# Attention layer: the products with the outputs' weights for two heads of both chunks at a time, in 64 columns

## The chip, the cores and the metric

The kernel runs on one core of one Trainium2 chip. Its time is the device time of one launch in microseconds (us), as the median of several runs. The engines of a core are TensorE (PE, with its weight loads shown apart as PEld), VectorE (DVE), ScalarE (ACT), GpSimd (POOL) and SyncE (SP, which here only issues DMA transfers). Each runs its own instructions in order; semaphores join them.

## The reference

Four graph layers follow one another on 6250 nodes of 160 features (64 scalars and 32 vectors of three components) and 100000 edges that are sorted by their destination. The change lies in the first, an attention layer. Cut to what matters:

```python
msg_s = (s_n @ Ws_src)[src] + (s_n @ Ws_dst)[dst]            # msg_v likewise
w1 = rbf @ W_rbf
m1_s, m1_v = _cg_tp(msg_s, msg_v, y0, y1, w1[...])            # products with the edge's y
a = (m1_s @ W_alpha).reshape(e, H, AS_)                       # H = 4 heads
a = jnp.sum(jnp.where(a > 0, a, 0.2 * a) * alpha_dot, axis=-1, keepdims=True)
amax = jax.ops.segment_max(a, dst, num_segments=n)
ex = jnp.exp(a - amax[dst])
den = jax.ops.segment_sum(ex, dst, num_segments=n)
alpha = ex / (den[dst] + 1e-16)
val_s = m1_s @ Ws_val                                         # val_v likewise; both gated by a sigmoid
m2_s, m2_v = _cg_tp(val_s, val_v, y0, y1, w2_...)
h = concat([m2_s @ Ws_vlin, m2_v @ Wv_vlin])                  # per head: 16 scalars, 8 vectors
agg = jax.ops.segment_sum(alpha * h, dst, num_segments=n)     # then a linear map, and a residual
```

## The kernel before, in words

The edges are padded to 784 chunks of 128. A chunk's edges reach few destination nodes: it has a window of 16 nodes (`WM0`). The edge loop of the attention layer, `edge_loop0`, takes four chunks (`WC0`) in each of its 196 steps. For every step there is an object of the class `Window0`, whose methods are the stages of the work; the list `STEP0` gives, for one step, pairs of a lag and a stage. In step s the stage with lag k is done for the chunks of step s - k. The list is written out in the code, and each engine gets its instructions in the list's order; so it is a pipeline of eight steps (lags 0 to 7). PSUM is shared out by `bank`: four banks in turn, 15 times a step, and a bank is given out again when the last reader of its tile is done.

The stages, in the order of the data:
- `edges` and `nodes` gather rows of features by edge and by window (POOL); `ends_load` and `radial_load` bring the destinations of the edges (tile `dn`), and their 16 radial features (`yr`) and factors (`yb`), for four steps at a time, as DMA transfers of SP. `radial_turn` multiplies the latter two (POOL), `masks` compares `dn` with the nodes of the windows (DVE), and `others` turns that into large negative numbers (ACT).
- `ends` and `weights` are products into the tile `wf`; `features`, `dots`, `dot` and `product1` form the message `tp` (DVE and POOL).
- `turn` and `turned` transpose it (PE, then a copy by ACT to `xt`); `linear` multiplies it with `w_m`; `tanh`, `directed`, `crossed`, `joined`, `gates`, `values` and `gated` form the values `val`.
- `channels`, `leak`, `leaky`, `scores` give the scores: a row of `s` for each head and node of a window, a column for each edge. Two chunks share 128 rows, ordered chunk, head, node (2 x 4 x 16). `largest`, `negated`, `exps` and `denominators` are the softmax.
- `by_edge` transposes the exponentials, `weighted` (L1473) multiplies them with the four factors of the edge. `sums` (L1481) and `sums_z` (L1493) sum the values over the edges, for each chunk, head, node and factor; ACT copies them out of PSUM as `a` (`summed`) and `az` (`summed_z`).
- `outputs` (L1512) multiplies `a` and `az` with the weights `w_o`. A product takes 32 columns of `a`, which are two heads of one chunk, as its stationary operand and 80 columns of weights (two heads side by side) as its moving one; five of them are summed into 32 rows of the tile `po`. There are 2 pairs of chunks x 5 x 2 chunks x 2 halves of the heads = 40 of them a step. `even` and `odd` pick the right head's 40 columns of the 80 into `row`.
- `write` (L1536) stores a chunk's rows of `row` to a table in DRAM, at its window's place, which `bases` (L1529) reads into registers of SP: one DMA for each chunk. After each step a part of the later layers' tables is filled with zeros (L1636, SP), as long as there are any left.

A product of 32-bit numbers is two instructions on PE with a weight load each, so a step's 40 products with `w_o` show as 80; transposes are one.

Of the kernel before, what the change touches and what calls it, by code (L numbers as in the profile page):

```python
# [10 lines left out]
F32 = mybir.dt.float32  # L11
I32 = mybir.dt.int32
# [21 lines left out]
ORDER0 = (0, 2, 1, 3)  # L34
# [13 lines left out]
def kernel(ctx: ExitStack, tc: tile.TileContext, t: dict, out: bass.AP):  # L48
# [146 lines left out]

    win0A = const.tile([1, NCH], I32, name="win0A")
# [5 lines left out]
    with tc.tile_pool(name="win", bufs=1) as sb, tc.tile_pool(name="winp", bufs=1, space=PSUM) as ps:  # L202
# [131 lines left out]
        bits = sb.tile([P, 3], I32, name="bits")  # L334
        vec.tensor_scalar(bits[:, 0:1], pi, 15, None, ALU.bitwise_and)
        vec.tensor_scalar(bits[:, 1:2], pi, 6, None, ALU.logical_shift_right)
        vec.tensor_scalar(bits[:, 2:3], pi, 4, 3, ALU.logical_shift_right, ALU.bitwise_and)
        bf = sb.tile([P, 3], F32, name="bf")
        vec.tensor_copy(bf, bits)
        vec.tensor_scalar(slot0[:, 0:1], bf[:, 1:2], float(WM0), bf[:, 0:1], ALU.mult, ALU.add)  # L340
# [11 lines left out]
        for h in range(2):  # L352
            q = slice(S * h, S * h + S)
            vec.tensor_copy(win0F[q, :], nb[q, h:NCH:2])
# [892 lines left out]
    class Window0:  # L1247
# [12 lines left out]
        def __init__(self, w, sb, ps, n, k, radial, dst, gi, y, yc, ids, node_idx, rows, tps):  # L1260
            self.w, self.sb, self.ps, self.n, self.np = w, sb, ps, n, n // 2
            self.k, self.radial, self.dst = k, radial, dst
            self.gi, self.y, self.yc, self.ids, self.node_idx = gi, y, yc, ids, node_idx
            self.rows, self.tps = rows, tps
            self.t, self.z, self.pa = {}, {}, {}
            self.f = self.xt = self.th = self.q = self.val = self.a = None

            self.groups = [(g, c) for g, c in enumerate(ORDER0) if c < n]

# [192 lines left out]
        def by_edge(self):  # L1462

            self.pe = self.bank()
            for p in range(self.np):
                pe.transpose(self.pe[:, p * P : (p + 1) * P], self.pT[:, p, :], ident)
# [16 lines left out]
        def summed(self, p):  # L1483
            if self.a is None:
                self.a = self.sb.tile([P, WC0, 4, S], F32, name="a", bufs=2)
            act.copy(self.a[:, 2 * p : 2 * p + 2].rearrange("p c i m -> p (c i m)"), self.pa[p])

        def sums_z(self):

            self.pz = pa = self.bank()  # L1490
            for c in range(self.n):
                for i in range(4):
                    pe.matmul(  # L1493
                        pa[i * V : (i + 1) * V, c * S : (c + 1) * S], self.val[:, c, P:F], self.py[:, c, i, :], start=True, stop=True
                    )

        def summed_z(self):
            n = self.n
            self.az = self.sb.tile([P, WC0, S], F32, name="az", bufs=2)
            act.copy(self.az[:, 0:n].rearrange("p c m -> p (c m)"), self.pz[:, 0 : n * S])  # L1500

        def outputs(self):

            w = self.w["o"]
            self.po = po = self.bank()[:, 0:160].rearrange("p (a k) -> p a k", a=2)
            for p in range(self.np):
                for i in range(5):
                    for h in range(2):
                        for g in range(2):
                            q = slice(h * S + g * 32, h * S + g * 32 + 32)  # L1510
                            x = (self.a[:, 2 * p + h, i, :] if i < 4 else self.az[:, 2 * p + h, :])[:, g * 32 : g * 32 + 32]
                            pe.matmul(po[q, p, :], x, w[:, i, g, :], start=i == 0, stop=i == 4)  # L1512
# [20 lines left out]
        def write(self, c):  # L1533
            q = slice(c % 2 * S, (c % 2 + 1) * S)
            k = self.rows[0][c]
            nc.sync.dma_start(tabs[0][k][0][:, ds(self.base[c], WM0), :], self.row[q, c // 2, :])  # L1536


        def radial_load(self):
            if self.k == 0:  # L1540
                self.radial.load()
# [9 lines left out]
    class Radial:  # L1551
# [3 lines left out]
        def __init__(self, sb, yb, parts, m):  # L1555
            self.sb, self.yb, self.parts, self.m = sb, yb, parts, m

        def load(self):
            m, yb = self.m, next(self.yb)
            self.y = yb  # L1560
            self.yr = yr = self.sb.tile([P, yb.shape[1], P], F32, name="yr", bufs=3)
            for g, (e, y) in self.parts.items():
                for h in range(2):
                    nc.sync.dma_start(yr[32 * g + 16 * h : 32 * g + 16 * h + 16, 0:m, :], e)
                nc.sync.dma_start(yb[32 * g : 32 * g + 16, 0:m, :], y.to_broadcast([16, m, P]))
# [6 lines left out]
    class Ends:  # L1572
# [5 lines left out]
        def load(self):  # L1578
            n = self.dst[0].shape[1]
            self.dn = self.sb.tile([P, self.m, P], self.dst[0].dtype, name="dn", bufs=2)  # L1580
            for h in range(2):
                nc.sync.dma_start(self.dn[h * S : (h + 1) * S, 0:n, :], self.dst[h].to_broadcast([S, n, P]))
# [4 lines left out]
        (7, "summed", 1), (4, "linear", 1), (0, "radial_load"), (4, "tanh", 1), (4, "linear", 3), (1, "edges", 0),  # L1587
        (5, "negated"), (3, "product1", 2), (4, "channels"), (1, "edges", 3), (4, "tanh", 3), (6, "denominators"),
        (4, "leak"), (4, "directed", 1), (5, "exps"), (7, "outputs"), (3, "turn", 3), (4, "directed", 3),
        (4, "leaky"), (5, "values"), (7, "even"), (3, "turn", 2), (4, "others"), (5, "by_edge"), (4, "crossed"),  # L1590
        (7, "odd"), (5, "gates"), (2, "ends"), (5, "weighted"), (4, "joined", 0), (3, "turned", 3),
        (3, "turned", 2), (2, "weights"), (3, "turn", 0), (3, "turned", 0), (3, "turn", 1), (2, "features"),
        (1, "edges", 1), (4, "scores"), (3, "bases"), (2, "dots"), (4, "largest"), (3, "turned", 1), (6, "sums", 0),
        (6, "summed", 0), (6, "sums_z"), (0, "ends_load"), (7, "write", 0), (3, "linear", 0), (5, "joined", 1),
        (3, "linear", 2), (6, "sums", 1), (2, "product1", 0), (2, "dot", 1), (2, "dot", 2), (1, "masks"),
        (3, "tanh", 0), (2, "product1", 1), (7, "write", 2), (7, "write", 1), (6, "summed_z"), (5, "gated"),
        (3, "tanh", 2), (0, "nodes"), (3, "directed", 0), (3, "directed", 2), (1, "edges", 2), (2, "product1", 3),
        (7, "write", 3), (0, "radial_turn"),
    ]

    def edge_loop0(w, res):
        with tc.tile_pool(name="sb0", bufs=1) as sb, tc.tile_pool(name="ps0", bufs=1, space=PSUM) as ps:
# [35 lines left out]
            ws, g0 = [], None  # L1638
            NST = NCH // WC0
            with tc.manual_schedule():  # L1640
                for s in range(NST + max(x[0] for x in STEP0)):
                    if s < NST:
                        c0 = s * WC0
                        if s % R == 0:
                            m = min(R, NST - s)
                            e = t["es16T"][:, c0 * P : (c0 + m * WC0) * P].rearrange("i (c p) -> i c p", p=P)
                            y = y_rows[c0 : c0 + m * WC0, :].rearrange("(o c) p -> o c p", o=1)
                            dst = t["dst_row"][0:1, c0 * P : (c0 + m * WC0) * P].rearrange("o (c p) -> o c p", p=P)
                            g0 = (
                                Radial(sb, yb, {g: (e[:, c::WC0, :], y[:, c::WC0, :]) for g, c in enumerate(ORDER0)}, m),  # L1650
                                Ends(sb, [dst[:, h::2, :] for h in range(2)], 2 * R),
                            )
                        q = slice(c0, c0 + WC0)
                        ws.append(
                            Window0(
                                w, sb, ps, WC0, s % R, *g0, [res["src"][:, c : c + 1] for c in range(c0, c0 + WC0)],
                                res["y"][:, q, :], res["yc"][:, q, :], win0F[:, 2 * s : 2 * s + 2], win0G[:, s : s + 1],
                                ([c % tab_n[0] for c in range(c0, c0 + WC0)], win0A[:, q]), tps,
                            )
                        )  # L1660
                    for lag, name, *arg in STEP0:
                        if 0 <= s - lag < NST:
                            getattr(ws[s - lag], name)(*arg)
# [3 lines left out]
        with ExitStack() as c2:  # L1667
# [27 lines left out]
            for c in range(CH):  # L1695
# [10 lines left out]
                for name in (  # L1706
# [5 lines left out]
                    "sums_z", "summed_z", "outputs", "even", "odd",  # L1712
# [47 lines left out]
    with ExitStack() as c0:  # L1760
        wp = c0.enter_context(tc.tile_pool(name="w0", bufs=1))
        with tc.tile_pool(name="nodes0", bufs=2) as sb, tc.tile_pool(name="nodes0p", bufs=2, space=PSUM) as ps:
# [53 lines left out]
            vec.memset(ad[0:S, 0:S], 1.0)  # L1816
            a4 = ad[0:S, 0:S].rearrange("k (h m) -> k h m", h=4)
# [12 lines left out]
            vec.tensor_scalar(ad[0:S, 0:S], ad[0:S, 0:S], ac, None, ALU.mult)  # L1830
            nc.sync.dma_start(ad[S:P, S:P], ad[0:S, 0:S])
# [269 lines left out]
```

## Time and profile before

| | |
|---|---|
| median of 11 runs | 8256.64 us (8246.79 to 8274.28) |
| the profiled execution | 8262.49 us; span in the profile 8259.1 us |
| busy share of the span | PE 83%, PEld 64%, DVE 60%, POOL 53%, ACT 43% |
| products with `w_o` (L1512) | first starts at 394.2 us, last at 2803.2 us |
| instructions | 172707, of them PE 60984 products |

A row of the costliest groups names the line, the engine, the operation, the tiles (out <- in), the shape and the count; behind the first bar stand the busy time in us and the mean of one in ns, behind the second the idle time of the engine just ahead of such instructions and what ended it. "issue" stands for time in which the engine waited for nothing that the profile shows. A row of the timeline has the start and the length in us. SPq is SP's queue of DMA issues: the length is that of the issue, not of the transfer. PEclk is the granted clock of TensorE as a share of the full one.

### The profile page before, as it was taken

The numbers are of one execution on the slowest core, as the hardware profiler recorded it, in microseconds if no ns is written. First come the engines' busy times: TensorE is split into PE (matmuls) and PEld (weight loads), VectorE is DVE, ScalarE is ACT, GpSimd is POOL, SyncE is SP. The second block draws the span as 40 slices with busy tenths as digits, with TensorE's granted clock in tenths as the row PEclk, the third lists the DMA queues.
The fourth block names the chain that finished last, engine by engine and source line by source line (L and its number), as shares of the span: only waits on it lengthen the run. The fifth ranks groups of instructions, "written<-read, shape, count | busy, mean of one in ns | idle before, by whom it ended". The sixth has DMA issues, their size and how long they took to land. (4 is left out here: it accounts for less than half of the span.)

```text
span 8259.1 us, 172707 instructions
## 1 busy us (share of the span) xinstructions
PE 6820.0 (83%) x60984; PEld 5297.1 (64%) x60984; DVE 4942.8 (60%) x12477; ACT 3563.0 (43%) x10875; POOL 4408.8 (53%) x4283
## 2 busy tenths in 40 slices
PE   2898989899888789999999996666666677777777
PEld 1677777777777569999999994344444454444446
DVE  5477777777777657777777774233333454444446
ACT  0244444444444445555555555333333332222224
POOL 0255555555555207777777771555555225555550
PEclk9999999999999859999999995788888888888888
DMA  3233333333222235555555554222222343333335
GB/s 135 83 97 97 98 96 97 97 96 100 57 57 56 68 105 101 101 99 101 99 100 102 98 80 149 61 63 64 64 62 63 114 135 83 81 81 82 81 83 214
DMA packets 669597, 763.72 MB, mean 92 GB/s; under 512 B 197530, under 2 KB 531515, under 8 KB 666907
## 3 DMA queue, kind: packets, MB, share of 16 engines
q0 software_dynamic: 239904, 294.05, 20.2%
q1 hardware_dynamic: 427642, 449.66, 17.6%
q8 instruction: 494, 8.09, 0.4%
q10 hardware_dynamic: 1152, 8.60, 0.3%
q14 instruction: 405, 3.31, 0.1%
HBM read 505.36 MB, written 246.53 MB: 91 GB/s over the span
## 5 line engine op out<-in xcount | busy, mean ns | idle before, releaser
L787 POOL DMA_INDIRECT f<-feat,r_src x2352 | 2296.0, 976 | 1765.4 <-issue 622.2
L1146 POOL DMA_INDIRECT tab<-o,scat x784 | 1343.0, 1713 | 442.8 <-ACT o L1145 319.9
L922 PE MATMUL pa<-pr,oy 128*128 128x321 f32 (+1 forms) x3136 | 1171.3, 513 | 15.1 <-ACT o L934 6.4
L931 ACT COPY o<-pa 32x96 f32<-32x96 f32 (+4 forms) x2358 | 549.2, 243 | 1202.3 <-remote 439.1
L872 PE MATMUL ww<-w,hid 64*128 64x192 f32 (+1 forms) x2088 | 358.3, 475 | 780.3 <-ACT hid L860 371.6
L922 PEld LDWEIGHTS pa<-pr,oy 128*128 128x128 f32 x3136 | 653.7, 213 | 420.2 <-issue 292.8
L1132 PE MATMUL pt<-same,tp 128*128 128x128 f32 x6272 | 895.4, 286 | 8.2 <-DVE tp L775 5.1
L872 PEld LDWEIGHTS ww<-w,hid 64*128 64x128 f32 x2088 | 245.7, 253 | 924.6 <-ACT hid L860 399.5
L1132 PEld LDWEIGHTS pt<-same,tp 128*128 128x128 f32 x6272 | 764.2, 192 | 25.3 <-PE pf L1116 16.3
L1134 ACT COPY xt<-pt 128x512 f32<-128x512 f32 x784 | 458.9, 585 | 526.1 <-PE pt L1132 520.0
L911 DVE TENSOR_TENSOR pr<-f,ww 128x384 f32<-128x384 f32 x131 | 72.7, 555 | 926.7 <-ACT wy L876 798.8
L1357 PE MATMUL m<-w_m,xt 128*128 128x128 f32 x4704 | 611.9, 280 | 13.6 <-ACT az L1500 8.0
L1143 PE MATMUL po<-ov,xt 128*128 128x32 f32 x4704 | 611.6, 267 | 0.0
L1357 PEld LDWEIGHTS m<-w_m,xt 128*128 128x128 f32 x4704 | 572.1, 192 | 44.8 <-ACT az L1500 9.2
L1143 PEld LDWEIGHTS po<-ov,xt 128*128 128x128 f32 x4704 | 588.3, 192 | 0.0
L907 DVE TENSOR_TENSOR pr<-f,ww 128x384 f32<-128x384 f32 x131 | 72.4, 553 | 813.7 <-remote 490.8
L1512 PE MATMUL m<-w_o,a 128*32 128x80 f32 x12544 | 381.5, 237 | 195.4 <-issue 194.5
L1512 PEld LDWEIGHTS m<-w_o,a 128*32 128x32 f32 x12544 | 287.3, 110 | 328.4 <-issue 300.2
L876 ACT ACTIVATE wy<-ww,r_y 128x96 f32<-128x96 f32 x784 | 195.5, 348 | 668.6 <-issue 661.4
L1372 DVE TENSOR_TENSOR q<-m,yc 128x192 f32<-128x192 f32 x784 | 277.7, 354 | 322.6 <-ACT th L1362 282.9
L1362 ACT ACTIVATE th<-m 128x96 f32<-128x96 f32 x784 | 195.7, 250 | 611.8 <-remote 253.0
L1350 ACT COPY xt<-m 128x384 f32<-128x384 f32 x784 | 338.3, 484 | 236.0 <-PE m L1345 221.1
(353 smaller groups left out, 14489.7 us busy)
## 6 DMA issues: line engine op xcount, KB each, us to landing
tab<-zeros SPq DMA_DIRECT2D x131, 512.0 KB
nodes<-in_src_row_dram SPq DMA_DIRECT2D x98, 512.0 KB
f<-feat,r_src POOLq DMA_INDIRECT x2352
tb<-tab SPq DMA_DIRECT2D x24, 1280.0 KB
dn<-in_dst_row_dram SPq DMA_DIRECT2D x98, 256.0 KB
e<-in_ef64T_dram SPq DMA_DIRECT2D x196, 128.0 KB
dn<-in_dst_row_dram SPq DMA_DIRECT2D x196, 128.0 KB
e<-in_ef64T_dram SPq DMA_DIRECT2D x261, 96.0 KB
```

The lines of the kernel that those rows point to most:

```text
L787: pool.indirect_dma_start(out=o, out_offset=None, in_=table, in_offset=bass.IndirectOffsetOnAxis(ap=idx, axis=0),)
L872: pe.matmul(self.ww[:, q, 0:wn], self.hid[k, c * P : (c + 1) * P], m, start=True, stop=True)
L922: pe.matmul(pa[:, 0:m], self.oy[:, q, :], self.pr[:, q, 0:m], start=c == 0, stop=c == self.ns[h] - 1)
L931: act.copy(o[q, at : at + e], pa[q, b0 * V : b0 * V + e])
L1132: pe.matmul(pt[:, k, :], self.tp[:, c, lo : lo + P], self.same[:, c, :], start=True, stop=True)
L1134: act.copy(self.xt, pt)
L1143: pe.matmul(po[:, 96 + i * V : 96 + (i + 1) * V], xt[:, 1 + i, :], w["ov"], start=True, stop=True)
L1146: pool.indirect_dma_start(out=self.tables[c % len(self.tables)], out_offset=bass.IndirectOffsetOnAxis(ap=self.scat[:, c : c + 1], axis=0), ...
L1350: act.copy(self.xt[:, :, c, :], self.t[c][:, 0 : 3 * P].rearrange("p (k e) -> p k e", k=3))
L1357: pe.matmul(z[:, k, :], self.xt[:, k, c, :], self.w["m"][:, k, :], start=True, stop=True)
L1372: vec.tensor_mul(q[:, 0:2], x[:, 1:3], turns)
L1512: pe.matmul(po[q, p, :], x, w[:, i, g, :], start=i == 0, stop=i == 4)
```

## The change

- The rows of a pair of chunks are ordered half of the heads, chunk, head, node, in place of chunk, head, node. So the destinations, the windows' nodes, the matrix `w_adot` of the scores and the place of each head in the table's rows follow that order, and chunk c of a step is in row group c of `wf`'s products (`ORDER0`).
- `by_edge` and the copies `summed` and `summed_z` reorder, so that `a` and `az` hold 64 columns in a row for two heads of both chunks. `outputs` is cut in two stages, one for a pair of chunks, of 5 x 2 products with 64 columns: 20 a step. `sums_z` is cut in two stages as well.
- `write` takes two DMAs of half the rows for each chunk, since a chunk's rows are no longer together: 8 a step in place of 4.
- `ends_load` takes four DMAs of 32 partitions in place of two of 64.
- `radial_load` brings, in each step, a quarter of what the next four steps need (three DMAs), in place of twelve DMAs in every fourth step; they are issued by ACT in place of SP.
- The list `STEP0` is another one: other lags (0 to 8) and another order.

```diff
-ORDER0 = (0, 2, 1, 3)
+ORDER0 = (0, 1, 2, 3)
...
     def by_edge(self):
         self.pe = self.bank()
         for p in range(self.np):
-            pe.transpose(self.pe[:, p * P : (p + 1) * P], self.pT[:, p, :], ident)
+            o = self.pe[:, p * P : (p + 1) * P].rearrange("p (h g m) -> p g h m", h=2, g=2)
+            pe.transpose(o, self.pT[:, p, :], ident)
...
     def summed(self, p):
         if self.a is None:
-            self.a = self.sb.tile([P, WC0, 4, S], F32, name="a", bufs=2)
-        act.copy(self.a[:, 2 * p : 2 * p + 2].rearrange("p c i m -> p (c i m)"), self.pa[p])
+            self.a = self.sb.tile([P, 2, 8, 2, 32], F32, name="a", bufs=2)
+        act.copy(self.a[:, p].rearrange("p k h m -> p h k m"), self.pa[p].rearrange("p (h k m) -> p h k m", h=2, k=8))
...
-    def outputs(self):
+    def outputs(self, p):
         w = self.w["o"]
-        self.po = po = self.bank()[:, 0:160].rearrange("p (a k) -> p a k", a=2)
-        for p in range(self.np):
-            for i in range(5):
-                for h in range(2):
-                    for g in range(2):
-                        q = slice(h * S + g * 32, h * S + g * 32 + 32)
-                        x = (self.a[:, 2 * p + h, i, :] if i < 4 else self.az[:, 2 * p + h, :])[:, g * 32 : g * 32 + 32]
-                        pe.matmul(po[q, p, :], x, w[:, i, g, :], start=i == 0, stop=i == 4)
+        if self.po is None:
+            self.po = self.bank()[:, 0:160].rearrange("p (a k) -> p a k", a=2)
+        for i in range(5):
+            for g in range(2):
+                x = self.a[:, p, 2 * i + g] if i < 4 else self.az[:, p, g]
+                pe.matmul(
+                    self.po[g * S : (g + 1) * S, p, :], x.rearrange("p h m -> p (h m)"), w[:, i, g, :], start=i == 0, stop=i == 4
+                )
...
     def write(self, c):
-        q = slice(c % 2 * S, (c % 2 + 1) * S)
         k = self.rows[0][c]
-        nc.sync.dma_start(tabs[0][k][0][:, ds(self.base[c], WM0), :], self.row[q, c // 2, :])
+        for g in range(2):
+            q = slice(g * S + c % 2 * 32, g * S + c % 2 * 32 + 32)
+            nc.sync.dma_start(tabs[0][k][0][2 * g : 2 * g + 2, ds(self.base[c], WM0), :], self.row[q, c // 2, :])
...
     def radial_load(self):
-        if self.k == 0:
-            self.radial.load()
+        for x, k in [(self.radial, k) for k in range(4)] * self.first + [(self.radial_next, self.k)]:
+            if x is not None:
+                x.load(k)
...
     # Radial.load, now for one chunk k of the four
-            for h in range(2):
-                nc.sync.dma_start(yr[32 * g + 16 * h : 32 * g + 16 * h + 16, 0:m, :], e)
-            nc.sync.dma_start(yb[32 * g : 32 * g + 16, 0:m, :], y.to_broadcast([16, m, P]))
+        for h in range(2):
+            nc.scalar.dma_start(self.yr[32 * k + 16 * h : 32 * k + 16 * h + 16, 0:m, :], e)
+        nc.scalar.dma_start(self.y[32 * k : 32 * k + 16, 0:m, :], y.to_broadcast([16, m, P]))
...
     STEP0 = [   # the new list; the old one is with the kernel above
+        (3, "dots"), (6, "joined", 0), (4, "turned", 1), (6, "values"), (5, "tanh", 1), (1, "edges", 2),
+        (0, "nodes"), (2, "radial_turn"), (6, "joined", 1), (2, "masks"), (5, "linear", 2), (6, "gated"),
+        (3, "others"), (8, "sums", 0), (5, "tanh", 2), (5, "directed", 1), (4, "linear", 3), (5, "directed", 2),
+        (5, "negated"), (3, "product1", 0), (4, "turn", 0), (8, "outputs", 1), (8, "summed", 0), (3, "dot", 1),
+        (4, "turned", 0), (8, "outputs", 0), (3, "dot", 2), (4, "tanh", 3), (3, "product1", 1), (8, "even"),
+        (3, "product1", 2), (4, "channels"), (5, "gates"), (4, "leak"), (3, "product1", 3), (4, "directed", 3),
+        (0, "edges", 3), (0, "ends_load"), (0, "edges", 1), (2, "ends"), (5, "crossed"), (8, "odd"),
+        (0, "radial_load"), (2, "weights"), (3, "turn", 3), (8, "write", 0), (4, "leaky"), (6, "by_edge"),
+        (3, "turned", 3), (4, "linear", 0), (7, "sums", 1), (4, "tanh", 0), (7, "denominators"), (7, "summed", 1),
+        (4, "scores"), (5, "exps"), (6, "weighted"), (7, "sums_z", 1), (2, "edges", 0), (7, "sums_z", 0),
+        (7, "summed_z"), (4, "directed", 0), (8, "write", 2), (8, "write", 3), (3, "turn", 2), (4, "largest"),
+        (3, "turn", 1), (4, "linear", 1), (2, "features"), (8, "write", 1), (3, "turned", 2), (1, "bases"),
     ]
```

## The prediction

> **What bounds the kernel now.** The slices come first: TensorE (PE) is busiest between about 390 and 2800 us, where the edge loop of the attention layer runs. The busy time by stage there:
>
> ```profile
> core 0: us, PE busy (x) PEld busy (x) DVE busy (x) ACT busy (x) POOL busy (x), PEclk, DMA share, GB/s
> ...
> 1350.00:1600.00 250.00, 224.53 (x3562) 181.25 (x3562) 189.03 (x614) 119.87 (x373) 143.37 (x184) 0.98 0.37 99
> ```
>
> PE is busy 90%, VectorE (DVE) 76%, POOL 57%, ScalarE (ACT) 48%. The missing tenth of PE shows in the costliest groups (busy, mean | idle before them, releaser):
>
> ```profile
> L1512 PE MATMUL m<-w_o,a 128*32 128x80 f32 x12544 | 381.5, 237 | 195.4 <-issue 194.5
> L1512 PEld LDWEIGHTS m<-w_o,a 128*32 128x32 f32 x12544 | 287.3, 110 | 328.4 <-issue 300.2
> ```
>
> Nearly all of PE's idle time stands before the products of `outputs` (L1512), and "issue" says that no other engine released it. PE's timeline shows two steps:
>
> ```profile
> 1501.14 1.03 PE L1481 MATMUL m<-py,val 128*128 128x256 f32 x4
> 1502.10 0.65 PE L1493 MATMUL m<-py,val 128*32 128x64 f32 x32
> 1502.68 1.60 PE L1357 MATMUL m<-w_m,xt 128*128 128x128 f32 x12
> ...
> 1506.42 0.65 PE L1415 MATMUL m<-xt,w_alpha 128*64 128x256 f32 x4
> 1507.01 0.62 PE L1512 MATMUL m<-w_o,a 128*32 128x80 f32 x23
> 1508.80 0.37 PE L1512 MATMUL m<-w_o,a 128*32 128x80 f32 x7 [1.18 <-issue]
> ...
> 1509.99 0.88 PE L1345 MATMUL m<-ident,tp 128*128 128x128 f32 x6
> ...
> 1518.88 0.76 PE L1512 MATMUL m<-w_o,a 128*32 128x80 f32 x32
> 1519.46 0.31 PE L1512 MATMUL m<-w_o,az 128*32 128x80 f32 x7
> ...
> 1523.32 0.88 PE L1345 MATMUL m<-ident,tp 128*128 128x128 f32 x6
> ```
>
> A step is 11.87 us (1507.01 to 1518.88). Its outputs block lasts 2.98 us, the next step's 4.44; the rest of the step is 8.89 (1509.99 to 1518.88), back to back. The block is 80 products and 80 weight loads. At full pace 32 of them take 0.58 us (1518.88 to 1519.46), 18 ns each, so 80 need 1.45; 1.5 us and more are holes. Everything else idles in them: DVE waits 2.11 us for a tanh of ACT that starts only at 1508.87. The 32 small products of L1493 pass with no hole. So I read: a dense run of some 50 to 90 PE instructions is fed, a run of 160 is not.
>
> L1512 first starts at 394.2 and last at 2803.2: 2409 us for 195 steps, 12.35 on average; without the five draining steps (34 us together) 12.5. Above 11.87 are every fourth step with its longer block, and stretches at lower granted clock.
>
> **The change, part by part.** PE: a step's outputs become 40 products of 64 columns in place of 80 of 32. Four 32-column products ran side by side in 4 x 18 = 72 ns; two of 64 columns stream the same 80 columns. If they run side by side too, the array time is the same 20 x 72 ns = 1.45 us, for half the instructions. That two halves run together shows in L1415: four half-width products of 256 columns take 0.59 us (1506.42 to 1507.01), while L1428 takes 0.43 for two full-width ones (1500.71 to 1501.14). The 0.16 left over is 0.08 a pair; charged to each of 20 pairs the block is 3.0 us, the upper end. The lower end is 40 x 18 ns = 0.72. I take 1.45, nearest to the line's own row, with the same depth and width, and 0.1 for entering the mode; leaving it is free, as `channels` (64 columns too) now follows.
>
> [...]
>
> The holes: 367 PE instructions in 11.87 us are 31 per us (180 products, 180 loads, some waits). After, a step has about 287; even at that rate they need 9.3 us, less than the array time, so I cost the holes at nothing. If this cover is wrong, 1.5 us per step come back.
>
> So a step's PE time is 8.89 + 1.45 + 0.1 = 10.44 us, against 12.5.
>
> The other engines, per step. DVE has the same instructions; weighted to weighted is 11.88 us (1499.24 to 1511.12) less its one hole of 2.11: 9.8. POOL is unchanged: 7.1 busy, and 0.3 between each of five gathers: 8.6. ACT is busy 48% of 12.5 = 6.0, with strided copies of the same size, and gains the radial loads: three a step, 0.45 each on SP (two L1564 in 0.89 us, L1565 in 0.37 to 0.52): 7.4. On SP those leave, but each write becomes two:
>
> ```profile
> 1512.82 4.40 SPq L1536 DMA_DIRECT2D tab<-row  x4
> 1517.26 0.59 SPq L1636 DMA_DIRECT2D tab<-zeros  x1
> 1524.14 3.01 SPq L1536 DMA_DIRECT2D tab<-row  x4
> 1527.19 0.45 SPq L1636 DMA_DIRECT2D tab<-zeros  x1
> ```
>
> A write costs 0.75 (3.01 / 4), after the dn loads 1.10 (4.40 / 4). Halved in size it may cost less, but yr, with as many descriptors as a write, still costs 0.45: eight are 3.6 to 8.8 us, and I take 6.0. With the register loads (2.0, the gap from 1509.09 to 1511.07), the zero fill (0.5) and four dn loads per four steps (at most 0.69 each, 0.7 a step) SP comes to 9.2. All lie below 10.44, so PE still sets the pace.
>
> The new order of the step list decides whether they fit between each other. By the order of instructions on each engine I followed what PE waits for, with the row's durations. PE's turn 0 needs directed 1 done, which DVE reaches some 1.2 us earlier; outputs need directed 2 (1.0 earlier); linear 1 needs `largest` (0.9 earlier); `outputs` 1 has its sums a step earlier, `outputs` 0 its copy 1.3 us earlier; the z sums need `weighted` (0.9 earlier). New on ACT: the three loads stand between `leak` and `turned` 3, and hold behind them tanh 0, `summed` 1 and the exponentials; tanh 0 is due on DVE about 0.5 us later. Each load waits first for an older transfer, mostly SP's writes of the step before, issued some 5 us earlier. I add 0.15 us for such waits: 10.6.
>
> **Sum.** 190 x (12.5 - 10.6) = 361 us. The pipeline is one step deeper; the seven steps before the first outputs took about 8 us each (338 to 394), so +8. The few operations added to the preparation and the weights run once, about 1 us each, below what is counted here. The profiled execution took 8262.5 us (span 8259.1), the median is 5.9 lower: 8262.5 - 353 - 5.9 = 7904.
>
> **The rivals.**
> 1. Another queue paces it: SP with writes at 1.10, or DVE and ACT in each other's way. For: DVE's 9.8 leaves 0.6. Against: the margins above. A step of 11.0 to 11.5 gives 7980 to 8075.
> 2. The change doesn't do what it says: the hole follows the place, not the count, or the 64-column pairs cost what L1415's do. For: holes begin after 23 products already, and 80 instructions are more than that. Against: L1493. A step of 11.5 to 11.9 gives 8075 to 8150.
> 3. Slower: ACT's loads wait for SP's writes, SP waits for the row that ACT and DVE finish, and the loop closes through both queues. Price: 8 x 1.25 + 2.0 + 0.5 + 0.7 = 13.2 us a step, 190 x 0.7 = 133 more: about 8400. It decides once a write costs over 1.16 us in every step (8 x 1.16 + 3.2 = 12.5). Against: 1.10 appears only behind dn loads.
>
> **How the numbers follow.** The forecast (7850 to 7960) has 0.60, rival 1 0.18, rival 2 0.11, rival 3 0.07, about no change 0.03, and 0.01 for below 7840 (a step of 10.25, nearer DVE's 9.8). The range 7840 to 8140 leaves out rival 3, no change and the tail of rival 2. A difference of 0.2% (17 us) is about what a measurement can tell. Faster: 0.60 + 0.18 + 0.11 + 0.01 = 0.90.
>
> **What would show it.** Right: the idle time of `outputs` by issue falls from about 195 us to below 30; its 40 products keep some 72 ns a pair; PE's steps are 10.4 to 10.8 us; DVE's hole for tanh is gone. Wrong: PE's idle time before the transposes or linears, released by ACT or DVE (rival 1, 3), ACT's loads over 1.5 us a step, holes of 0.7 us within L1517's products (rival 2), or a step above 11 us.

## The result: 7.3% slower, and what the profile after shows

The changed kernel took 8867.61 us (median, 8854.1 to 8882.04) beside 8262.89 us for the kernel before: a ratio of 1.0731 [1.0719, 1.0744]. The prediction was 7904.

Nearly all of the loss lies in the edge loop of the attention layer. The profiled execution has a span of 8873.9 us against 8259.1, 614.8 more. The products of `outputs`, now L1517, first start at 409.1 us and last at 3407.4, so the loop takes 2998.3 us where it took 2409.0: 589.3 more. The other 25 are 14.9 ahead of the first products and 10.6 behind the last. The busy time by stage, in the columns of before (window, length, PE, PEld, DVE, ACT, POOL, PEclk, DMA share, GB/s):

```profile
1350.00:1600.00 250.00, 225.51 (x2282) 174.37 (x2282) 159.51 (x504) 100.32 (x309) 119.81 (x148) 0.88 0.28 77
```

PE still shows 90% busy, but DVE has fallen from 189.03 to 159.51, and PE's granted clock from 0.98 to 0.88. Over 700 to 2300 us PE ran at half clock for 30.1% of the time (3.6% before). The groups by shape:

```profile
L1306 PE MATMUL wf<-w_rbf,yr 32*128 32x224 f32 x1568 | 316.7, 507 | 25.2 <-issue 16.1
L1517 PE MATMUL m<-w_o,a 128*64 128x80 f32 x6272 | 287.7, 236 | 0.0
L1301 PE MATMUL wf<-fw,on 16*128 16x160 f32 x1568 | 261.3, 385 | 97.3 <-issue 84.2 <-DVE tp L1328 5.0 <-DVE q L1384 4.3
...
L1419 PE MATMUL m<-xt,w_alpha 128*64 128x256 f32 x784 | 238.6, 414 | 143.7 <-issue 132.8 <-ACT xt L1354 3.2
L1517 PE MATMUL m<-w_o,az 128*64 128x80 f32 x1568 | 150.9, 234 | 41.0 <-issue 33.3 <-DVE q L1384 1.6 <-DVE q L1378 0.4
...
L1524 ACT ACTIVATE row<-m,own 128x80 f32<-128x80 f32 x196 | 64.3, 328 | 1059.7 <-PE wf L1301 782.9 <-PE m L1419 133.3 <-remote 121.9
```

The idle time has left the outputs, nearly as forecast: 214.4 us before L1512 (195.4 and 19.0 for its two tiles), 41.0 before L1517 (33.3 of it by issue). But it has gone to what now follows them, `channels` (L1419) and `ends` (L1301). The row to stop at is the last one. `even` needs only the products of `outputs`, yet it waits 1059.7 us, 5.4 a step, and the engine named is not PE at those products but PE at work that comes behind them. The timeline shows why:

```profile
1509.12 0.98 POOL L790 DMA_INDIRECT f<-feat,r_src  x1 [0.15 <-issue]
...
1509.91 0.77 PE L1517 MATMUL m<-w_o,a 128*64 128x80 f32 x16
...
1510.40 0.96 POOL L790 DMA_INDIRECT f<-feat,r_src  x1 [0.30 <-issue]
...
1511.21 0.30 PE L1517 MATMUL m<-w_o,az 128*64 128x80 f32 x2
...
1511.67 0.95 POOL L790 DMA_INDIRECT f<-feat,r_src  x1 [0.30 <-issue]
...
1512.35 0.23 PE L1517 MATMUL m<-w_o,az 128*64 128x80 f32 x1 [0.84 <-issue]
...
1513.07 0.23 PE L1517 MATMUL m<-w_o,az 128*64 128x80 f32 x1 [0.50 <-issue]
1513.52 0.97 POOL L790 DMA_INDIRECT f<-feat,r_src  x1 [0.16 <-issue]
...
1513.79 2.15 PE L1419 MATMUL m<-xt,w_alpha 128*64 128x256 f32 x4 [0.49 <-issue]
...
1514.79 0.94 POOL L790 DMA_INDIRECT fw<-feat,win0G  x1 [0.30 <-issue]
...
1516.92 0.33 ACT L1524 ACTIVATE row<-m,own 128x80 f32<-128x80 f32 x1 [6.27 <-PE m L1419]
```

38 of the 40 products go by in 1.4 us (1509.91 to 1511.3), most of them 69 ns a pair. Then PE creeps: in this step the next products start 0.72 us apart, be they of 80 columns or of 256; in others the distances vary (in the median step 15 products start in 3.6 us, where without the stop 180 start in 10.4). `even`, whose input was all issued by 1513.1, starts at 1516.92. Beside it stand POOL's five gathers of the step, one after the other, 1.27 us apart but for one `joined` between the third and the fourth.

The trace also holds the events that raise PE's semaphore; not every product raises it. In this step one arrives at 1509.998 and the next at 1516.897; between them DVE, ACT and POOL have five, the last at 1513.38. From 600 to 2300 us 105 of 108 steps hold such a run of five gathers. The longest stretch without such an event, called a completion below, is 6.47 us there in the median, and it ends 1.73 us after the last of the five has started (1.68 to 2.01 in 8 of 10 steps), whether that gather comes 4.3 or 4.9 us after the first product. Not all of the stretch is lateness, since outputs run in it; the lateness shows in `even`, which starts 4.60 us (median) after the last product that it needs has started.

In the trace of before the gathers stand elsewhere:

```profile
1503.09 0.97 POOL L787 DMA_INDIRECT fw<-feat,win0G  x1 [0.23 <-PE m L1493]
...
1506.86 0.95 POOL L787 DMA_INDIRECT f<-feat,r_src  x1 [0.30 <-issue]
```

These are the first and the last of a run of four, 1.25 to 1.27 us apart, which ends just as the outputs begin (1507.01). In the 100 steps with such a run the stretch is 2.87 us and ends 1.93 us after its last gather. So my hole of 1.5 us in L1512 was, by its place, the tail of this. The longer block of every fourth step, which the prediction noted and did not ask about (4.44 us from 1518.88), belongs to it too: three gathers start there between 1518.63 and 1521.78, and the stretch of 5.04 us ends 1.65 us after the third.

Gathers alone do not cost, though. In the kernel before, the first three of the four stand beside the large products of L1357 and L1481, and a step without its outputs takes 8.89 us in the median, as much as in `few_before` below, where three of the gathers are missing and no stop was met. So it also counts what PE does beside them. In the profiles with the stop PE starts a few dozen more products after the last completion before its first pause of over 0.45 us, where there is one (median 34 before, 41 in the changed kernel and in `spread`). A dense stage would get there sooner than one of large products; that explanation is argued, no run tries it. The trace speaks against the loading of code as the cause: 44 of the 108 longest stretches hold no packet of instructions.

I call this the stop: PE's completions cease during a run of gathers, and its products creep. It is not in every execution: in some of the comparisons below the kernel before took 8181 to 8192 us (8263 in the first), in others 7139 to 7141, and one comparison has only the one or the other, so each result is told with the time of the kernel before that stood beside it.

### The profile page after: what moved, and what is told of

It reads as the page before. It is cut to its first block, busy times and chain, and to the rows that moved or that the text cites. A ratio compares the mean times of both kernels' runs of the same rounds, so it can differ in the third digit from the quotient of the medians.

```text
span 8873.9 us, 159892 instructions
## 1 busy us (share of the span) xinstructions
PE 7376.8 (83%) x53144; PEld 5665.2 (64%) x53144; DVE 5005.9 (56%) x12481; ACT 3583.7 (40%) x10875; POOL 4466.5 (50%) x4283
## 5 line engine op out<-in xcount | busy, mean ns | idle before, releaser
L1339 POOL TENSOR_TENSOR d<-d 128x128 f32<-128x128 f32 x392 | 238.9, 609 | 1317.0 <-DVE d L1335 1301.6
L1361 PE MATMUL m<-w_m,xt 128*128 128x128 f32 x4704 | 725.4, 305 | 5.1 <-issue 1.4
L1361 PEld LDWEIGHTS m<-w_m,xt 128*128 128x128 f32 x4704 | 687.4, 220 | 20.3 <-DVE row L1528 5.4
L1528 DVE SCALAR_TENSOR_TENSOR row<-m,own,row 128x80 f32<-128x80 f32 x196 | 59.1, 301 | 788.7 <-ACT row L1524 780.2
L1486 PE MATMUL m<-py,val 128*128 128x256 f32 x1568 | 497.6, 449 | 0.0
L1524 ACT ACTIVATE row<-m,own 128x80 f32<-128x80 f32 x196 | 64.3, 328 | 1059.7 <-PE wf L1301 782.9
L1354 ACT COPY xt<-m 128x384 f32<-128x384 f32 x784 | 356.3, 480 | 296.1 <-PE m L1349 174.6
```

Source lines behind the costliest of these rows:

```text
L1339: pool.tensor_add(d[:, :, 0, :], d[:, :, 0, :], d[:, :, j, :])
L1354: act.copy(self.xt[:, :, c, :], self.t[c][:, 0 : 3 * P].rearrange("p (k e) -> p k e", k=3))
L1361: pe.matmul(z[:, k, :], self.xt[:, k, c, :], self.w["m"][:, k, :], start=True, stop=True)
L1486: pe.matmul(pa[:, h * 256 : (h + 1) * 256], self.val[:, c, 0:P], py, start=True, stop=True)
```

## The experiments

Theory A: the stop is caused by POOL's runs of gathers; the new list `STEP0` makes the run longer and puts it over outputs, channels, ends and weights. Theory B: it is caused by the products themselves, a dense run of small ones. Theory C: the new order makes the queues wait for each other, whatever the gathers do. A and B do not exclude each other: the stop could need both the gathers and a dense run.

| kernel | stop present: beside 8181 to 8192 us | stop absent: beside 7139 to 7141 us |
|---|---|---|
| changed (`same_again`) | not met again; first result 1.0731, beside 8263 | 7159.01, 1.0030 [1.0019, 1.0042] |
| `spread` | 8119.08, 0.9933 [0.9906, 0.9960] | 7161.98, 1.0031 [1.0019, 1.0042] |
| `few_after` | 7819.51, 0.9556 [0.9529, 0.9584] | 7123.44, 0.9978 [0.9968, 0.9987] |
| `few_before` | not met | 7131.75, 0.9992 [0.9982, 1.0001] |
| `products` | not met | 7143.56, 1.0008 [0.9999, 1.0018] |
| `order` | not met | 7145.99, 1.0006 [0.9997, 1.0016] |
| `double` | 9017.77, 1.1008 [1.0960, 1.1056] | not met |
| `double_before` | 8482.62, 1.0355 [1.0325, 1.0385] | not met |

Repeats with the stop absent gave `spread` 1.0026 to 1.0035, `few_after` 0.9978 and 0.9984, `order` 1.0010, `products` 1.0012.

### The same program without the stop

Nothing is edited here (`same_again`).

> The changed kernel as it is, once more, beside the kernel before. In the last four runs the kernel before took 7139 us and not 8263, and runs of gathers as long as those of the first profiles (five starts 1.27 us apart) stood beside a TensorE that went on. Theory A1 (the stop behind a run of gathers is a condition of the first measurements, not of the program): where the kernel before takes 7139 us the changed one has no long stop, a step near the 10.1 to 10.3 us of the two runs with its products, 7120 to 7200 us, ratio 0.997 to 1.008; where the kernel before takes 8263 us it takes 8868 us again. Theory C (the new order itself costs the time): ratio 1.07 either way, 7640 us beside 7139.

The kernel before took 7139.6 us beside it and the changed one 7159.01. Theory A1 (in the expectation above) holds and theory C falls: the same instructions in the same order cost 0.3%, not 7.3%. Its groups and its timeline:

```profile
L1517 PE MATMUL m<-w_o,az 128*64 128x80 f32 x1568 | 121.0, 233 | 0.0
L1419 PE MATMUL m<-xt,w_alpha 128*64 128x256 f32 x784 | 118.2, 380 | 2.3 <-ACT xt L1354 2.3
L1306 PE MATMUL wf<-w_rbf,yr 32*128 32x224 f32 x1568 | 111.8, 352 | 5.0 <-POOL yr L1585 5.0
L1301 PE MATMUL wf<-fw,on 16*128 16x160 f32 x1568 | 109.8, 349 | 27.1 <-DVE on L1288 10.1 <-issue 9.5 <-DVE tp L1328 7.5
...
L1524 ACT ACTIVATE row<-m,own 128x80 f32<-128x80 f32 x196 | 64.4, 329 | 184.9 <-PE m L1517 146.5 <-issue 34.7 <-PE m L1419 2.7
```

```profile
1504.91 0.95 POOL L790 DMA_INDIRECT f<-feat,r_src  x1 [0.30 <-issue]
...
1505.66 0.31 PE L1517 MATMUL m<-w_o,az 128*64 128x80 f32 x4
...
1505.80 0.60 PE L1419 MATMUL m<-xt,w_alpha 128*64 128x256 f32 x4
...
1506.02 0.33 ACT L1524 ACTIVATE row<-m,own 128x80 f32<-128x80 f32 x1 [0.91 <-PE m L1517]
1506.17 0.95 POOL L790 DMA_INDIRECT f<-feat,r_src  x1 [0.30 <-issue]
```

`even` is now released by PE at L1517, 0.28 us after the last of its products has started (as in the median step), with gathers at the same pace on both sides of it. The longest stretch without a completion is 1.55 us in the median, which is the block of outputs itself. `channels` take 0.60 us in place of 2.15. Set side by side, L1517's `az` products, L1419, L1301 and L1306 cost in busy and idle time 779.5 us more with the stop (70.9 + 261.8 + 221.7 + 225.1), 4.0 us of the 5.3 by which a step is longer (15.7 on average against 10.4, from one `weighted` to the next).

### Three of four gathers left out

```diff
     def edges(self, c):
...
-        gather(self.f[:, c, :], feat[0][:, :], self.gi[c])
+        if c == 0:
+            gather(self.f[:, c, :], feat[0][:, :], self.gi[c])
+        else:
+            pool.memset(self.f[:, c, :], 0.0)
```

On the changed kernel (`few_after`), first where the stop was absent, and in the end where it was present:

> The changed kernel with only chunk 0 of four gathered; `edges` 1 to 3 fill their rows with zeros on POOL instead (that part of the computation is left out). Two gathers a step are left, not next to each other. Theory A: no stretch of over 2 us without a completion of TensorE, the idle time of `even` (ACT row L1524) falls from 1060 us to below 200, the step to 10.5 to 11.5 us, the time to 7990 to 8180 us. Theory B: the break behind the products stays, 8800 to 8900 us. Theory C: 8700 to 8870 us (a little for POOL's shorter work).

7123.44 us beside 7139: the expectation supposed a stop, and there was none; so the edit itself saves the changed kernel some 36 us. Then, beside 8181.25:

> The changed kernel with three of its four gathers of `edges` replaced by zeros (that part is left out). Where the kernel before takes about 8200 us: theory A step 10.1 to 10.5 us, no stop of over 2 us in the loop, 7750 to 7900 us (the layers behind it keep their gathers and their part of the loss); theory B 8700 to 8850. Where it takes 7139 us: 7125 as three times before.

7819.51 us, within theory A's bounds; theory B's lower end is 880 us away. The group of `even` (L1527 here) and the stage:

```profile
L1527 ACT ACTIVATE row<-m,own 128x80 f32<-128x80 f32 x196 | 64.3, 328 | 179.6 <-PE m L1520 178.6 <-DMA tab<-row 1.0
```

```profile
1350.00:1600.00 250.00, 245.10 (x3363) 208.06 (x3362) 233.23 (x745) 147.59 (x457) 124.45 (x223) 0.99 0.33 93
```

The wait of 1059.7 us is 179.6, the step 10.4 us (10.3 for the same kernel without the stop), the longest stretch without a completion 1.54 in the median. It is over 2 us in 24 of 164 steps, mostly 2.54 (8 of 163 in `same_again`). The products, their order and the other engines' work are those of the changed kernel, apart from POOL's zeros in place of features, so in this loop the stop needs the gathers; the dense products alone do not bring it. What is left of the loss, 7817.7 against 7120.1 us of span, is behind the loop, in layers that keep their runs of twelve gathers.

On the kernel before (`few_before`):

> The kernel before with the same part left out (three of four gathers replaced by zeros). Theory A: the 195 us of idle time by issue before the products of L1512 fall below 60 though their number and their 32 columns stay; step 10.5 to 11 us, 7890 to 8000 us. Theory B (the hole is that of 160 dense instructions): the 195 us stay, 8200 to 8260 us.

7131.75 us beside 7139: it met no stop, so it tells nothing of A. PE was busy 300 us of 300 in this loop at a step of 10.42 us, with 80 products of 32 columns: 160 dense instructions (products and loads) are fed without a hole.

### More products, with the stop present

Each product of `outputs` made twice, in both kernels; the second pass writes the same values again.

```diff
-            for i in range(5):
+            for i in [0, 1, 2, 3, 4] * 2:
```

> The kernel before with its 80 products of outputs made twice: 160 products of 32 columns, 320 instructions in a row. Theory A1: 18 to 19 ns each, block 3.0 us, no holes, 7140 + 196 x 1.45 = 7420 us. Theory B: the run is three times as long as what was fed, holes of 3 us and more per step, over 8000 us. Where the kernel before takes 8263 us: 8400 to 8600.

> The changed kernel with each of its 40 products of outputs made twice (the second pass writes the same values over the first): 80 products, 160 instructions in a row. If TensorE sets the pace where the kernel before takes 7139 us, and a pair costs the 72 ns of my prediction, the block grows from 1.43 to 2.87 us, the step from 10.4 to 11.8, the time by 196 x 1.4 = 270 us to about 7430 us, with no holes (theory A1). Theory B: holes of 1 us and more come back in the run of 160, over 7600 us. Where the kernel before takes 8263 us: the stop hides part of it, 8900 to 9150.

Beside 8191.9 us the first took 8482.62 and the second 9017.77. The kernel before, doubled:

```profile
L1512 PE MATMUL m<-w_o,a 128*32 128x80 f32 x25088 | 693.2, 235 | 206.7 <-issue 202.4
...
L1512 PE MATMUL m<-w_o,az 128*32 128x80 f32 x6272 | 314.0, 235 | 3.8 <-issue 3.5
```

Twice the instructions, and the idle time before them is 210.5 us, where the kernel before, in the same comparison, has 198.7 (and 214.4 in the first profile). With `few_after` this rules out theory B by itself, and my reading of the hole: it doesn't grow with the run. The extra products cost 313 us by the spans (8480.5 against 8167.6), 1.60 us a step or 20 ns each; A1 had 18 to 19, and its 7420 us supposed that the stop would be absent; for the stop 8400 to 8600 was written, without a theory. `double` costs 0.0277 more than the changed kernel's ratio, 227 us or 1.2 a step, less than the 1.4 of the products themselves. The rest may lie inside the stop: the block of outputs now takes 6.96 us in the median, and the rest of the step 9.70, where the first result has 1.74 and 13.92. The stretch is 7.46 us and ends 2.64 us after the last gather has started, so the 1.73 of above is no constant. Both theories had written 8900 to 9150 for that case, so it doesn't tell them apart.

The kernel before as it is stood in the same comparison (`before_again`):

> The kernel before as it is, for its profile where it takes 7139 us. Theory A1 (on the first chip TensorE stops beside runs of gathers, on these it does not): the runs of gathers are there as in the first profile, the 195 us of idle time by issue before L1512 are gone (below 10), the block of outputs is 1.5 us in place of 3.0, the median step 10.2 to 10.5 us. Theory B (a dense run of 160 instructions is not fed): the holes stay, and something else is 1100 us shorter.

It took 8170.39 us, with 187.5 and 11.2 us idle before L1512's two tiles, so it is a second profile of the stop and not the one without it that was wanted; the kernel before has no profile without the stop.

### The run of gathers parted

`spread` is the changed kernel with all five gathers of a step; their place in the list differs, and `joined` and `edges` 0 come one step earlier.

```diff
-        (3, "dots"), (6, "joined", 0), ... (1, "edges", 2), (0, "nodes"), ... (6, "joined", 1), ...
+        (3, "dots"), ...
...
-        (0, "edges", 3), (0, "ends_load"), (0, "edges", 1), (2, "ends"), (5, "crossed"), (8, "odd"),
+        (0, "edges", 3), (0, "ends_load"), (0, "edges", 1), (2, "ends"), (5, "crossed"),
+        (5, "joined", 0), (1, "edges", 2), (0, "nodes"), (5, "joined", 1), (1, "edges", 0), (8, "odd"),
...
-        ... (2, "edges", 0), ...
```

> The changed kernel with POOL's five gathers of a step taken apart: `joined` 0 and 1 move directly behind `crossed` (lag 5), and `edges` 2, `nodes` and `edges` 0 stand around them, so that two gathers follow `dot` 2 and three the `crossed` of DVE. Theory A (TensorE's completions stop during a run of back-to-back gathers on POOL, and come again some 1.7 us after the last one of the run has begun): the longest stretch without a completion falls from about 6.3 us to 3.5 or less, the step from 15.1 to 12 to 13 us, the time to 8270 to 8470 us. Theory B (a dense run of small products needs its break wherever the gathers are) and theory C (the new order of the step list alone makes the queues wait for each other): no change, 8830 to 8910 us.

Without the stop it took 7161.98 us beside 7139, like the changed kernel. With it, beside 8184.8:

> The changed kernel with POOL's run of five gathers parted into two and three, all kept, as before. Where the kernel before takes about 8200 us: theory A stops of 2 to 3 us in place of 6.5, step 12 to 13.5 us, 8150 to 8500 us; rival (the number of gathers sets it, wherever they stand) step 15 us, 8700 to 8850 us. Where it takes 7139 us: 7162 us again.

8119.08 us, 0.9933 [0.9906, 0.9960] of the kernel before, a little better than theory A's range; the rival (the number of gathers, wherever they stand) has its lower end 580 us away. Its slices of the granted clock on the page, and its `even`:

```profile
PEclk9999999999999669999999995888888888888888
```

```profile
L1524 ACT ACTIVATE row<-m,own 128x80 f32<-128x80 f32 x196 | 64.4, 329 | 180.4 <-PE m L1517 167.1 <-PE m L1419 9.0 <-PE wf L1301 2.3
```

The run of five in a row, 6.47 us without a completion, is now a run of three with 2.91 in the median and a run of two with 1.80. The step is 11.9 us against 15.7. It stays above the 10.4 without the stop: between 700 and 2300 us PE is idle by issue for 81.4 us before L1349 and 46.8 before L1499, which now stand beside the gathers. The edit shortens the runs and moves them off the outputs at once, so it does not tell which of the two counts; in the kernel before a run of three came with 5.04 us and runs of four with 2.87, so the length alone does not set the stretch.

Half clock in the loop (700 to 2300 us) is down to 0.6% from 30.1%. What brings it is not shown here; the length of the stretches alone does not set it: in `spread` one step in ten still has a stretch of 5.05 us or more, and `double`, with 7.45 in the median step, has 18.1% of half clock, where the changed kernel has 30.1% with 6.47. Since products start inside the stretches, their length is not idle time.

`spread` beats both kernels where the stop is present (0.9933 against 1.0731, each against the kernel before of its own comparison). Where it is absent it loses the same 0.3% as the changed kernel, so no version here beats the kernel before in both cases.

### The parts of the change without the stop

`products` is the changed kernel with the old list, `outputs` 0 and 1 side by side:

```diff
-    STEP0 = [ the new list ]
+    STEP0 = [ the old list, with (7, "outputs", 0), (7, "outputs", 1) and (6, "sums_z", 0), (6, "sums_z", 1) ]
```

> The changed kernel with the step list of the kernel before (its order and lags), `outputs` 0 and 1 next to each other, `sums_z` too: the new products, the row layout, eight writes and the radial loads on ACT stay. Theory A: the run of gathers is as long as before (four, ending just as the outputs begin), so the hole of about 1.5 us stays, behind or in the outputs; step 12 to 12.5 us, 8150 to 8270 us. Theory B as my prediction had it (fewer instructions, no hole): 7900 to 8000 us; theory B as rival (64-column products need the longer break): 8800 us. Theory C: 8150 to 8270 us as A.

`order` is the kernel before with the new list, `outputs` and `sums_z` at the places of their second halves:

```diff
-    STEP0 = [ the old list ]
+    STEP0 = [ the new list, with (8, "outputs") for "outputs" 0 and 1, (7, "sums_z") for "sums_z" 0 and 1 ]
```

> The kernel before with only the new step list (its order and lags; `outputs` stands where `outputs` 0 does and `sums_z` where `sums_z` 0 does): old products of 32 columns, four writes, radial loads on SP. Where the kernel before takes 7139 us: theory C (the list costs the 0.3% of the changed kernel, products and layout nothing) 7150 to 7170 us; theory B (the products cost it) 7130 to 7145. Where it takes 8263 us: theory A (the list puts a run of five gathers over outputs, channels, ends and weights, TensorE stops behind it) 8700 to 8950 us, a stop of about 6 us in each step; theory B (the 64-column products bring the stop) 8200 to 8350.

Neither met a stop, so A against B wasn't tried by them. Without it each part is about 0.1% above the kernel before, 4.4 and 6.5 us (11.3 and 6.6 in the repeats below), while both together cost 19.4. So C's price is not in the list alone; the intervals are some 7 us wide to either side, and whether the two parts add up to the whole is not settled. The row of `order`:

```profile
L1512 PE MATMUL m<-w_o,a 128*32 128x80 f32 x12544 | 294.6, 234 | 3.2 <-ACT a L1486 2.7 <-issue 0.3
```

The old products with no hole: 80 of 32 columns take 1.52 us a step, the 40 of 64 in `same_again` 1.43. Steps average 10.43 us in `order`, `products` and `same_again` alike, with PE busy 97 to 99% and DVE 91 to 93% of the window of 1350 to 1600 us.

### Repeats that did not meet the stop

The kernels are those above; each repeat fell on a comparison without the stop and gives its earlier time again. `spread`:

> The changed kernel with POOL's five gathers of a step taken apart (two behind `dot` 2, three behind `crossed`), a second time, for a chip on which TensorE's completions stop beside gathers. Where the kernel before takes 7139 us: 7162 us again. Where it takes 8263 us: theory A 8270 to 8470 us, theories B and C 8830 to 8910 us.

> The changed kernel with POOL's run of five gathers parted into two and three. On a chip where the kernel before takes about 8200 us: theory A (the stop lasts from the third gather of a run until 1.7 us after the last has begun) stops of 2 to 3 us in place of 6.5, step 12 to 13.5 us, 8150 to 8500 us; theory B (the 64-column products bring the stop, wherever the gathers are) 8800 to 8900. Where the kernel before takes 7139 us: 7160 as twice before, and nothing is told apart.

> The changed kernel with POOL's run of five gathers parted into two and three, all of them kept. Where the kernel before takes about 8200 us: theory A (the length of the run sets the stop, about 1.27 us for each gather after the second) stops of 2 to 3 us in place of 6.5, step 12 to 13.5 us, 8150 to 8500 us. Rival (the number of gathers sets it, wherever they stand): the same 6 us of standing still in sum, step 15 us, 8700 to 8850 us. Where the kernel before takes 7139 us: 7162 us as before, and nothing is told apart.

7159.70, 7164.47 and 7164.66 us. `few_after`:

> The changed kernel with three of its four gathers of `edges` replaced by zeros (that part is left out), a second time, for the same reason. Where the kernel before takes 7139 us: 7123 us again. Where it takes 8263 us: theory A no stop of over 2 us, 7400 to 8180 us (the other layers keep their gathers); theories B and C 8700 to 8900 us.

> The changed kernel with three of its four gathers of `edges` replaced by zeros (that part is left out). Where the kernel before takes about 8200 us: theory A step 10.1 to 10.5 us, no stop of over 2 us in the loop, 7750 to 7900 us (the layers behind it keep their gathers and their part of the loss); theory B 8700 to 8850.

7124.36 and 7125.77 us. `order` and `products`:

> The kernel before with only the new step list. Where the kernel before takes about 8200 us: theory A (the list makes a run of five gathers and puts it over outputs, channels and ends) 8700 to 9000 us, a stop of about 6 us in each step; theory B (the products bring it) 8200 to 8300.

> The changed kernel with the old step list (outputs next to each other, four gathers in a run as before). Where the kernel before takes about 8200 us: theory A a stop of 2 to 3 us as before, step 12 to 12.6 us, 8100 to 8250 us; theory B 8700 to 8900.

7145.17 and 7149.87 us. What the list alone and the products alone do where the stop is present is therefore still open.

## Why the prediction was wrong

**The step that failed** is "so I cost the holes at nothing", with what it stood on: "a dense run of some 50 to 90 PE instructions is fed, a run of 160 is not". The length of the run does not set the hole: 160 instructions go without a hole where there is no stop, and 320 have the same hole as 160 where there is one (210.5 us against 198.7). By its place the hole in L1512 was the end of PE's stop beside POOL's gathers; that it goes when they go was shown for the changed kernel's loop (`few_after`), not for the kernel before. So halving the instructions could not be counted on to take it away, and the 1.9 us a step that I counted as gain was not the products' to give.

**What made it slower** is the next step in the same part, "POOL is unchanged". Its work is; its place isn't. The new list was followed only for what PE waits for. The gathers, which it lets run one after the other across outputs, channels, ends and weights, got no term, since they waited for nobody and nobody for them. With the run of five the stretch without completions went from 2.87 to 6.47 us, and half clock came on top (30.1% of the time between 700 and 2300 us, 3.6% before). `spread` shows with the changed products that the placing does this; the new list with the old products was not met with the stop.

**The terms that held** are those of the array, read without the stop: block 1.45 us forecast, 1.43 measured; PE's step 10.44 forecast, 10.09 in the median and 10.43 on average measured. They bring nothing: without the stop the kernel before takes 7139.6 us beside 7159.01, and `order`, which has its products, has the same step of 10.4 us (the kernel before has no profile there). That the array time would be the same for half as many products of double width was right up to 0.09 us a step: 1.52 for the 80 of 32 columns in `order`, 1.43 for the 40 of 64 in `same_again`. The rate of PE's instructions in the trace of before, 31 per us or 66 ns for each of the 180 products (11.87 us), was no bound: the 180 of a step of `order` take 10.22 us in the median, 57 ns each. The 0.1 us for entering the mode is there: in the changed kernel's trace the first product of L1517 starts 0.20 us after the last transpose (L1349), where transposes start 0.11 apart (medians between 700 and 2300 us). Behind the block nothing is added: in `same_again` `channels` start 0.14 us after the first of the last four products of outputs (1505.66 to 1505.80), and inside the block the next products 0.14 us after the first of the four `az` products before them (1504.97 to 1505.11).

**The rivals.** The second, "the hole follows the place, not the count", came nearest in its first half, but its price stopped at giving back 1.5 us: a hole that can move can also grow, and for that there was no upper end. The third had the sign and the wrong mechanism: SP's eight writes took 6.75 us in a step (my 6.0), 0.84 each and well below the 1.16 from which it was to decide, and ACT's loads are there in `same_again` too, at a step of 10.4:

```profile
1503.02 6.75 SPq L1544 DMA_DIRECT2D tab<-row  x8
```

The loads on SP again, by themselves, were not tried.

Of the signs of being right that I named, idle time of `outputs` by issue below 30 nearly came true (33.3) and "DVE's hole for tanh is gone" all but did (189.6 us of waits for it between 700 and 2300 us before, 24.1 after), while the kernel got slower: they looked only at the place where the hole had been. Of the signs of being wrong, "a step above 11 us" came (15.7), and it named no cause.

## What to carry to other kernels

Idle time by "issue" is a question, not a cause: look at what the other engines do in each such stretch, and ask at which of their events it ends, over all steps; if the end keeps a fixed distance from another engine's instruction, edit that one. When a list is reordered, give the engine that waits for nothing a term too, above all POOL's gathers: keep runs of them short and off PE's dense stages (`spread` did both at once: with the stop it took 0.9933 of the kernel before, the changed kernel 1.0731). And where a wait lasts past the work that it waits for, read when completions arrive and not only when instructions start.

## What the runs showed of the hardware

- PE's completions can cease for some 6 us beside back-to-back indirect gathers of POOL, while its products creep (15 starts in 3.6 us). Five gathers, mostly 1.27 us apart, do it (6.47 us in the median), and in the layer behind it that gathers again, with runs of twelve, the stretches are some 10 to 11 us in the median (4.0 where the stop is absent). Single gathers in `few_after` do not (1.54), and three in a row beside large products cost nothing (8.89 us for the rest of the step either way).
- The same program has this in some executions and not in others: 8868 and 7159 us. The difference lies in the loops that gather rows of `feat` one after the other; the layer between them took 1851.5 us both times, from its first L1097 to its last, though POOL issues 784 indirect writes there. The gathers' own durations are alike (977 and 984 ns), and their DMA packets take no longer with the stop (288 ns for 4480 B in the median, 312 without). Two chip numbers appeared on both sides, so it isn't simply the chip. What else it is, and how the gathers reach PE, stays open.
- A loss of 7.3% and a loss of 0.3% are thus both true of this change, and neither carries over to the other condition.
